# Four fused layers on one Trainium2 core: how the attention loads its images and weights, takes its first split, and places two steps of its plan

## The chip, the core and the metric

The kernel runs on one core of one Trainium2 chip. A core has a matrix engine (TensorE, PE in the profile), a vector engine (VectorE, DVE), an engine for activation functions (ScalarE, ACT), a general engine (GpSimd, POOL) and one that mostly issues transfers (SyncE, SP). SP, ACT and POOL each have a queue of DMAs, written SPq, ACTq and POOLq. Every engine works through its own instructions in order and waits on semaphores for the others. The metric is the device time of one execution in microseconds (us), lower is better: the median of three runs.

## What is computed

Four layers in a row on x of 8 images x 256 channels x 32 x 32 pixels. Layer 0 is an attention with a batch norm ahead of it and a small network behind it; layers 1 to 3 are convolutions, two of them deformable. The change touches layer 0's attention alone. Cut to that:

```python
NH, KD, D = (16, 16, 64)              # heads, width of q and k, width of v
y = _bn(xf, g1, b1)                   # mean and variance over all images and pixels
q = einsum('bcn,oc->bon', y, wq) + bq          # 256 outputs: 16 heads of 16
k = einsum('bcn,oc->bon', y, wk) + bk
v = einsum('bcn,oc->bon', y, wv) + bv          # 1024 outputs: 16 heads of 64
attn = softmax(einsum('bhnk,bhkm->bhnm', q, k) / KD ** (-0.5), axis=-1)
o = einsum('bhnm,bhmd->bhnd', attn, v)
xf = xf + einsum('bdn,od->bon', o, wp) + bp    # then batch norm, MLP, layers 1 to 3
```

Since the batch norm takes its mean and variance over all eight images, no projection can begin before the last image is there.

## The kernel before, in words

**Start.** Eight DMAs on SP's queue (L169) load one image of 1 MB each. vec, the packed small parameters, comes on ACT's queue (L176), and behind it wq and wk (L241): the host stores each head's 16 columns padded to 32, and the DMA takes only the 16, so its pieces have 64 bytes. Behind these are the biases of q and k (L253), 32 DMAs of 16 numbers each out of vec's memory. DVE forms each image's statistics (L284), 32 instructions of 512 columns, then the norm's scale and shift (L205 to L217, with a root on ACT, L213). wv follows on ACT's queue (L287), wp and bv on POOL's (L288, L289).

**First group.** From L621 on, the order of PE, ACT, DVE and POOL is written out by hand; SP's DMAs go where the program's text has them, as a rule. Four pieces project q and k of image 0 (L326), ACT adds the bias (L338) and rounds to bf16 (L340), both are written to memory, and rows are copied into the q and k tiles (L630). Then four pieces of values (L381, copied by L385). Then the split: each of q and k is cut into three bf16 levels whose sum is the number. The difference to level 0 is taken in place (L349), rounded to level 1 (L354), and the difference of that is level 2 (L356). The `split` calls stand behind all four value pieces (L631 to L635). The levels go through memory and are loaded as stacks of rows, `stack` (L364), 16 loads for each of two head pairs. The first block finds its score maxima in another way, with 32 matmuls on q and k themselves (L411) and 32 reductions (L414).

**The steady state.** A group is four heads of one image; there are 32 groups, and two blocks in each, one for each half (h) of the queries. A block takes eight steps, so a group takes 16; step t0 is a group's first. A step has, for the block in work: four score matmuls (L443) with exponentials on ACT (L444, in buffers e, six of them, which L440 takes), two pairs of value matmuls (L455), and two sums of exponentials on POOL (L463, L465). It also finds maxima for a block eleven steps ahead: eight bf16 matmuls on the stacks (L398) and four reductions on DVE (L402).

**The plan.** All other work is put by `plan(step, place, f, ...)` into a step and one of three places in it; `step` (L601) plays them out. For the next group, `project_v` makes value pieces at t0 + 0, 1, 2 and 4, `stack` loads pair 0 at t0 + 1 to 3 and pair 1 at t0 + 5 to 7, and `spread` (L370) loads q and k at t0 + 9 to 12. A pair's stack is one buffer, so its loads wait until the maxima of the pair that used it are done. In groups of even number there are also `project_qk` at t0 + 8 to 14 and `split` at t0 + 10 to 18, for the group after next (q and k of two groups are projected together). For a finished block with t1 = its end: `total` (L476) sums over keys at t1 + 3, `invert` (L486) takes the reciprocal in four parts, `lay` (L494) copies them to where they are needed with eight DMAs (r), `scale` (L499) multiplies on POOL, and `add_projected` (L529, added on DVE by L535 or L537) applies wp at t1 + 13 and 15. `enter_max` (L420 to L431) writes a block's maxima into q's spare rows. For h = 1, where t1 is the t0 of the next group, before the change:

```python
plan(t1_ + ((4, 5, 6, 8) if h == 0 and n + 2 < nblk else (4, 4, 5, 6))[i], 0, invert, m, i)
at = 8 if h == 0 and n + 2 < nblk else 6
plan(t1_ + at, 2, lay, m)
plan(t1_ + at + 2, pair, scale, m, pair)
```

## Time and profile before

| what | value |
|---|---|
| median of three runs | 4313.98 us (4313.37 to 4317.53) |
| the profiled execution's own time | 4320.31 us |
| its span | 4318.5 us |
| PE / DVE / ACT / POOL busy | 3989.3 / 3037.9 / 1859.1 / 3312.7 us |
| granted PE clock, mean | 0.971 |
| first matmul of a projection | 48.24 us after the span's start |
| first value matmul of an attention step | 108 us |
| attention's end | about 2700 us |

How to read it: the page has one row for each engine with its busy time, then the span in 40 slices (a digit is tenths of a slice), DMA queues, the chain of work that ended last, and groups of instructions by line. Other views of the same trace are a timeline (start, duration, engine, line, operation, tiles, and in brackets the idle time ahead of it with what ended it), waits in total, and stretches of time with each engine's busy time. A line such as L398 is a line of the kernel; numbers in the profile of the changed kernel stand a few lines further down.

### The profile page before, as it was taken

The page shows a single profiled execution, that of the slowest core. Times are in us where ns is not written, and L with a number is a line of the kernel's source. Part 1 is how long each engine was busy: PE and PEld are TensorE (multiplying, and loading weights), DVE is VectorE, ACT ScalarE, POOL GpSimd, SP SyncE. Part 2 cuts the span into 40 slices and gives each one's busy share as a digit, 9 for nine tenths or more (in the row PEclk, how much of TensorE's full clock was granted, in tenths as well). Part 3 has the DMA queues.
Part 4 walks back from the last instruction along what each step waited for, and adds up shares of the span by engine and source line. Part 5 has one row for each costly group of instructions (what it writes and reads, how often), then busy time and mean ns, then how long its engine had stood idle before and what let it go on. Part 6 is the DMA issues. An engine that isn't in the chain of part 4 may idle for free.

```text
span 4318.5 us, 60323 instructions
## 1 busy us (share of the span) xinstructions
PE 3989.3 (92%) x20959; PEld 1546.3 (36%) x20959; DVE 3037.9 (70%) x5148; ACT 1859.1 (43%) x3329; POOL 3312.7 (77%) x2022
## 2 busy tenths in 40 slices
PE   4999999999999999999999999999899977999976
PEld 1333333333333333333333333344334433444432
DVE  5667777767767777777677676657777764777665
ACT  1545545545545555555455454423223223444321
POOL 1888888888888988888888888447777771489767
PEclk8999999999999999999999999999999998999988
DMA  5211212222122122122122121124344442000000
GB/s 156 64 53 57 71 52 64 64 54 70 56 58 71 53 60 69 55 57 75 51 61 70 52 61 50 47 77 121 115 120 120 121 129 80 5 10 15 15 15 21
DMA packets 215834, 282.59 MB, mean 65 GB/s; under 512 B 96336, under 2 KB 126560, under 8 KB 215264
## 3 DMA queue, kind: packets, MB, share of 16 engines
q1 hardware_dynamic: 177104, 199.12, 16.1%
q0 software_dynamic: 28720, 77.90, 6.0%
q8 instruction: 168, 2.75, 0.3%
q10 hardware_dynamic: 9696, 1.62, 0.2%
q14 instruction: 146, 1.20, 0.1%
HBM read 180.55 MB, written 63.82 MB: 57 GB/s over the span
## 4 chain that ended last, share of the span: by engine, by line
PE 66%; DVE 13%; POOL 7%; issue 5%; DMA 3%; SPq 3%; ACT 2%; ACTq 0%; DVEq 0%; POOLq 0%
PE av L455 18%; PE pb L398 11%; PE sc L443 10%; POOL g L876 5%; PE pb L381 5%; PE pc L1173 5%; PE pa L1357 2%; PE pb L529 2%; PE pb L326 2%; PE po L756 2%; DMA g<-table,idx 2%; SPq L494 2%; PE pm L743 2%; DVE pm L402 2%; DVE r L486 2%
## 5 line engine op out<-in xcount | busy, mean ns | idle before, releaser
L465 POOL TENSOR_TENSOR esum<-esum,e 128x1024 f32<-128x1024 f32 x762 | 1812.6, 2413 | 57.1 <-ACT e L444 56.5
L402 DVE TENSOR_REDUCE pm<-pb 128x1 f32<-128x512 f32 x2016 | 1355.1, 684 | 662.9 <-PE pb L398 658.4
L444 ACT ACTIVATE e<-sc 128x512 f32<-128x512 f32 x2048 | 1057.2, 602 | 721.4 <-PE sc L443 713.7
L455 PE MATMUL av<-e,v 128*64 128x512 f32 x4096 | 1061.6, 597 | 0.0
L398 PE MATMUL pb<-sk,sq 128*64 128x512 bf16 x4032 | 776.0, 388 | 85.0 <-DMA sk<-lev_d 30.5
L876 POOL DMA_INDIRECT g<-table,idx x576 | 551.0, 957 | 257.0 <-issue 160.7
L398 PEld LDWEIGHTS <-sq 128*64 128x64 bf16 x4032 | 267.4, 109 | 942.9 <-issue 929.0
L443 PE MATMUL sc<-q,k 32*128 32x512 f32 x4096 | 593.5, 642 | 0.7 <-ACT e L444 0.7
L463 POOL TENSOR_TENSOR esum<-e 128x1024 f32<-128x1024 f32 x127 | 302.9, 2406 | 191.9 <-ACT e L444 191.9
L455 PEld LDWEIGHTS av<-e,v 128*64 128x64 f32 x4096 | 298.1, 138 | 211.4 <-issue 120.8
L1365 POOL TENSOR_TENSOR part<-part,pr 128x512 f32<-128x512 f32 x224 | 289.7, 1295 | 66.6 <-DVE pr L1351 55.4
L1351 DVE TENSOR_TENSOR pr<-pw,v 128x512 f32<-128x512 f32 x400 | 257.9, 682 | 106.5 <-PE pw L1346 60.3
L1173 PE MATMUL pc<-xpad,wc 128*128 128x512 f32 x576 | 277.8, 609 | 4.1 <-ACT h L1178 4.1
L499 POOL TENSOR_TENSOR o<-r,o 128x512 f32<-128x512 f32 x126 | 158.8, 1271 | 153.5 <-DMA r<-r 82.1
L529 PE MATMUL pb<-o,wp 128*64 128x512 f32 x1024 | 246.0, 599 | 3.8 <-POOL o L499 3.3
L443 PEld LDWEIGHTS sc<-q,k 32*128 32x128 f32 x4096 | 164.9, 183 | 233.1 <-issue 187.3
L743 PE MATMUL pm<-y,wide 128*128 128x512 f32 x512 | 238.9, 611 | 6.2 <-DVE y L717 5.8
L756 PE MATMUL po<-hid,w 128*128 128x512 f32 x512 | 240.3, 616 | 1.8 <-DVE x L760 1.7
L381 PE MATMUL pb<-wide,y 128*64 128x256 f32 x2048 | 241.8, 379 | 0.0
L486 DVE RECIPROCAL r<-r 128x128 f32<-128x128 f32 x252 | 233.2, 936 | 0.0
L385 ACT COPY v<-pb 128x512 f32<-128x512 f32 x128 | 75.0, 586 | 266.7 <-PE pb L381 266.7
L898 DVE TENSOR_TENSOR near_p<-g,near_p 128x320 f32<-128x320 f32 (+1 forms) x384 | 177.6, 462 | 13.2
(250 smaller groups left out, 3921.2 us busy)
## 6 DMA issues: line engine op xcount, KB each, us to landing
sq<-lev_d SPq DMA_DIRECT2D x512, 64.0 KB
r<-r SPq DMA_DIRECT2D x504, 64.0 KB
sk<-lev_d SPq DMA_DIRECT2D x496, 64.0 KB
lev_d<-lev SPq DMA_DIRECT2D x180, 128.0 KB
u_d<-u SPq DMA_DIRECT2D x60, 256.0 KB
g<-table,idx POOLq DMA_INDIRECT x576, 2.7
x<-in_x SPq DMA_DIRECT2D x8, 1024.0 KB
table<-v SPq DMA_DIRECT2D x32, 256.0 KB
```

The costliest lines, as they stand in the source:

```text
L381: nc.tensor.matmul(ps[c * 64 : (c + 1) * 64, (mt % 2) * 256 : (mt % 2 + 1) * 256], ys[b][:, t, k0 : k0 + 64], wv[:, t, g * 256 : (g + 1) * ...
L398: nc.tensor.matmul(ps[c * 64 : (c + 1) * 64, :], sq[pair][:, c, q0 : q0 + 64], sk[pair][:, c, kh * HALF : (kh + 1) * HALF], start=True, st ...
L402: nc.vector.tensor_reduce(maxima[m][:, pair, qt, kh : kh + 1], ps, AX.X, ALU.max)
L443: nc.tensor.matmul(ps, k[r, kt * P : (kt + 1) * P], q[r, h * HALF : (h + 1) * HALF], start=True, stop=True)
L444: nc.scalar.activation(es[m, kt, j // 2][:, j % 2, :], ps, AF.Exp)
L455: nc.tensor.matmul(av[i * HD : (i + 1) * HD, :], vss[b, g][:, kt, j * HD : (j + 1) * HD], e[:, i, :], start=kt == 0, stop=kt == NT - 1,)
L465: eng.tensor_add(sums[m, pair], sums[m, pair], es.pop((m, kt, pair)))
L529: nc.tensor.matmul(ps[c * 64 : (c + 1) * 64, :], wp[:, 2 * g + i, o0 : o0 + 64], outs[(b, g, h), i], start=i == 0, stop=i == 1,)
L743: nc.tensor.matmul(ps, w1[:, t, i * P : (i + 1) * P], ys[b, h][:, t, :], start=t == 0, stop=t == 1)
L756: nc.tensor.matmul(pss["o", b, h, t], w2[:, j, t * P : (t + 1) * P], hids[b, h, j], start=j == 0, stop=j == 7)
L876: nc.gpsimd.indirect_dma_start(out=g[:, k, :], out_offset=None, in_=tables[b][:TR, :], in_offset=bass.IndirectOffsetOnAxis(ap=idxs[b][:, t ...
L1173: nc.tensor.matmul(S["c", b, h], wc[:, t, k, :], tap(xpads[t], k, H // 2, h * H // 2), start=t == k == 0, stop=t == 1 and k == 8,)
```

## The change

1. Images: 16 DMAs of half an image (128 channels, 0.5 MB), those of the first half of the channels on SP's queue, those of the second half on ACT's.
2. wq and wk are loaded whole, with the padding, into two e buffers, behind the images (wq on SP, wk on ACT); ACT copies out the 16 columns of each head, two copies each.
3. Biases of q and k: in place of 32 DMAs and a multiplication on DVE, eight matmuls of one column pick the rows out of vec (with `taken`, the identity's columns without the padding, copied by POOL), and ACT writes the two tiles with the scale.
4. wv, wp and bv are issued in the hand-written part, after `normed`.
5. First split: the difference goes into the other half of its buffer (`rest`) instead of over u; its stage 0 follows each projection piece, stages 1 and 2 each value piece.
6. Odd groups make their fourth value piece at t0 + 9 instead of t0 + 4.
7. For h = 1 (all such blocks but the very last, which has a path of its own), reciprocals go to t1 + 4, 5, 6, 7 (before 4, 4, 5, 6), `lay` to t1 + 8 (before 6), `scale` to t1 + 10 (before 8).

```diff
     for b in range(B):
-        nc.sync.dma_start(x[:, :, b, :], x_in[b].rearrange("(t p) h w -> p t (h w)", p=P))
+        for t in range(2):
+            eng = nc.sync if t == 0 else nc.scalar
+            eng.dma_start(x[:, t, b, :], x_in[b, t * P : (t + 1) * P].rearrange("p h w -> p (h w)"))
...
-        for dst, name in ((wq, "wqT"), (wk, "wkT")):
-            src = d[name].rearrange("(t p) (n r) -> p t n r", p=P, r=32)
-            for t in range(2):
-                nc.scalar.dma_start(dst[:, t, :].rearrange("p (n r) -> p n r", r=KD), src[:, t, :, 0:KD])
...
-        for dst, name in ((bq4, "bq"), (bk, "bk")):
-            for c in range(4):
-                src = d["vec"][:, COL[name] + c : COL[name] + c + 1].rearrange("(n r) o -> n r o", r=32)
-                for j in range(4):
-                    r0 = (c % 2) * 64 + j * KD
-                    nc.scalar.dma_start(dst[r0 : r0 + KD, c // 2 : c // 2 + 1], src[j, 0:KD, :])
-        nc.vector.tensor_scalar_mul(bq4, bq4, 4.0)
...
+        for dst, name, eng in ((wq, "wqT", nc.sync), (wk, "wkT", nc.scalar)):
+            padded = ep.tile([P, 2, HALF], F32, name="e")
+            eng.dma_start(padded, d[name].rearrange("(t p) o -> p t o", p=P))
+            for t in range(2):
+                src = padded[:, t, :].rearrange("p (n r) -> p n r", r=32)[:, :, 0:KD]
+                nc.scalar.copy(dst[:, t, :].rearrange("p (n r) -> p n r", r=KD), src)
+        taken = w.tile([P, 4, KD], F32, name="taken")
+        nc.gpsimd.tensor_copy(taken, ident.rearrange("p (n r) -> p n r", r=32)[:, :, 0:KD])
+        for dst, name, scale in ((bq4, "bq", 4.0), (bk, "bk", 1.0)):
+            ps = ps_p.tile([P, 512], F32, name="pb")
+            for c in range(4):
+                nc.tensor.matmul(
+                    ps[c % 2 * 64 : c % 2 * 64 + 64, c // 2 : c // 2 + 1], taken.rearrange("p n r -> p (n r)"), col(name, c),
+                    start=True, stop=True,
+                )
+            nc.scalar.mul(dst, ps[:, 0:2], scale)
...
-                u = ep.tile([P, 2, HALF], F32, name="e")[:, 0, :]
+                both = ep.tile([P, 2, HALF], F32, name="e")
+                u, rest = both[:, 0, :], both[:, 1, :]
...
-                nc.vector.tensor_sub(u, u, lev[0])
+                nc.vector.tensor_sub(rest, u, lev[0])
...
-                    plan(t0 + (0, 1, 2, 4)[i], 1, project_v, *nxt, i)
+                    plan(t0 + (0, 1, 2, 9 if n % 2 else 4)[i], 1, project_v, *nxt, i)
...
+                at = 6 if n + 2 == nblk else 8
                 for i in range(4):
-                    plan(t1_ + ((4, 5, 6, 8) if h == 0 and n + 2 < nblk else (4, 4, 5, 6))[i], 0, invert, m, i)
-                at = 8 if h == 0 and n + 2 < nblk else 6
+                    plan(t1_ + ((4, 4, 5, 6) if at == 6 else (4, 5, 6, 8) if h == 0 else (4, 5, 6, 7))[i], 0, invert, m, i)
...
+            nc.scalar.dma_start(wv, d["wvT"].rearrange("(t p) o -> p t o", p=P))
+            nc.gpsimd.dma_start(wp, d["wpT"].rearrange("(t p) o -> p t o", p=P))
+            nc.gpsimd.dma_start(bv, d["bv"].rearrange("(t p) -> p t", p=P))
             for i in range(4):
                 project_qk(0, 0, i)
...
+                split(0, 0, i, 0)
             for i in range(4):
                 project_v(0, 0, i)
-            for i in range(4):
-                for k in range(3):
-                    split(0, 0, i, k)
+                split(0, 0, i, 1)
+                split(0, 0, i, 2)
```

## The prediction

> **What bounds the kernel now.** I read the 40 slices first: TensorE (PE) is at 9 tenths through the attention (the first 25 slices, to about 2700 us) except in slice one. So a gain must come from the start, where PE has nothing to do, or from PE's own waits. Next, the waits of the DMA queue of SyncE (SP) in the first 120 us: "who waits <- for what: us in total, times, longest".

> ```profile
> SPq L169 <- DMA wq<-in_wqT: 12.2, 1, 12.2
> SPq L169 <- DMA bq<-in_vec: 11.7, 2, 6.8
> SPq L169 <- DMA bk<-in_vec: 6.1, 2, 5.2
> ```

> The image loads stand still for transfers that have nothing to do with them[...]. The timeline of the same stretch (start, us, engine, line, tile; in brackets the idle time before):

> ```profile
> 14.66 12.32 ACTq L253 DMA_DIRECT2D bq<-in_vec  x16
> 27.02 11.28 ACTq L253 DMA_DIRECT2D bk<-in_vec  x16
> 43.09 2.47 DVE L284 BATCH_NORM_STATS2 stats<-x 128x6 f32<-128x512 f32 x4 [1.23 <-DMA x<-in_x]
> 48.24 3.30 PE L326 MATMUL pb<-y,wq 128*64 128x512 f32 x8 [48.24 <-DVE y L310]
> ```

> 32 bias loads of 16 numbers fill the ACT queue up to 38.3; the last image is seen at 43.09 and PE starts at 48.24. After that the first split and the first maxima:

> ```profile
> 56.65 0.69 DVE L349 TENSOR_TENSOR e<-e,esum 128x512 f32<-128x512 f32 x1 [7.09 <-DMA q<-e]
> 64.14 0.62 ACT L354 CAST esum<-e 128x512 bf16<-128x512 f32 x1
> 64.79 0.69 DVE L356 TENSOR_TENSOR esum<-e,esum 128x512 bf16<-128x512 f32 x1 [7.45 <-ACT esum L354]
> 71.33 0.68 DVE L414 TENSOR_REDUCE pm<-sc 128x1 f32<-128x512 f32 x1
> ```

> VectorE (DVE) waits 7.45 us because L354 stands behind four value copies on ACT, then alternates with ACT until 71.3; only then do the maxima begin. The table of stretches (length, busy us of PE, weight loads, DVE, ACT, POOL; granted clock, DMA share, GB/s):

> ```profile
> 71.33:93.84 22.51, 20.96 (x57) 7.21 (x58) 19.93 (x34) 0.66 (x1) 7.22 (x15) 0.50 0.66 111
> 108.20:2690.00 2581.80, 2498.65 (x15890) 916.42 (x15890) 1864.97 (x2905) 1314.73 (x2481) 2214.42 (x991) 1.00 0.21 60
> ```

> The maxima run at half clock. In the long stretch PE is 97% busy, GpSimd (POOL) 86%, DVE 72%. PE's own waits there, largest first:

> ```profile
> PE pb L398 <- DMA sk<-lev_d: 30.5, 16, 2.9
> PE pb L398 <- DVE x L537: 23.4, 44, 1.6
> PE pb L398 <- DVE pm L402: 13.2, 15, 1.8
> ```

> 16 waits for stacked keys, one for every second group. One of them, on SP's queue, PE and POOL:

> ```profile
> 395.40 0.42 SPq L364 DMA_DIRECT2D sk<-lev_d  x1
> 396.14 5.00 SPq L494 DMA_DIRECT2D r<-r  x8
> 401.18 0.58 SPq L364 DMA_DIRECT2D sq<-lev_d  x1
> ...
> 403.68 0.43 SPq L364 DMA_DIRECT2D sk<-lev_d  x1
> ```

> ```profile
> 406.39 0.41 PE L398 MATMUL pb<-sk,sq 128*64 128x512 bf16 x2 [1.36 <-DMA sk<-lev_d]
> ```

> ```profile
> 400.20 1.27 POOL L499 TENSOR_TENSOR o<-r,o 128x512 f32<-128x512 f32 x1 [2.70 <-PE pb L398]
> 402.69 1.26 POOL L499 TENSOR_TENSOR o<-r,o 128x512 f32<-128x512 f32 x1 [1.22 <-PE pb L398]
> ```

> Eight r transfers (the row sums' reciprocals) take SP 5.0 us just ahead of the last six stacking loads; PE wants them at 405.0 and gets them at 406.4. POOL idles 2.70 + 1.22 us for r as well: the releaser named, PE, is done long before, and r has just been issued.

> [...] two queues for the images give no bandwidth; the trace agrees (358 GB/s at 5 to 10 us with all queues, 401 GB/s at 40 to 45 with images alone). [...] The trace agrees with the fall (PE idle from 65.4 to 72.7, half clock from 68.1), but PE filled 93% of the maxima at half clock and did not get it back until 109.

> **The change, part by part.**

> *Images and weights.* 32 bias loads and the four element-wise weight loads go; 16 image loads of 0.5 MB, eight on each queue, come first, then vec, wk and wv behind them on ACT, wq on SP. [...] Bytes up to the last image: 8.39 MB and 1.05 MB of wp on POOL's queue; at 390 GB/s (between 358 and 401) 24.2 us. The first slice of 5 us moved 201 GB/s, so data starts at about 2.5: last byte at 26.7. An image of 1 MB took 4.80 us from the queue to the statistics at 38.26, of which 2.6 is data: I add 1.6, 28.3. But vec, before at the head of its queue, is now behind the images, and in DVE's new order bn_s (L186) stands ahead of the last six statistics: vec 28.5, table load 1.28 and L185 0.30: 30.1; then six statistics of 0.60 and eight small ones of about 0.07: 34.3; from statistics to PE as before, 48.24 - 45.56 = 2.7: PE at 37.0 instead of 48.2, **-11.2**. Bounds: -15 (vec not late) and -7 (340 GB/s). ACT's new work ahead of the batch norm's root: wq and wk land 1.05 MB later, 31.0; four copies (half the 0.62 of the 128x512 cast, an estimate) to 32.4, two small ones to 33.0; the root is wanted at 35.3. Hidden with 2.3 us to spare; weights later than that push PE by the same amount. Eight matmuls of one column run on an idle PE, the picking copy on an idle POOL: nothing. wv lands near 34, wanted at 45.

> *First split.* "rest" takes the other half of the buffer, so DVE no longer waits for the readers of e, and ACT casts after each value copy. ACT has its last projection piece at S+9.9 (S is PE's start; 58.09 before); the value copies follow PE at 1.73 us, the last ends at S+16.0, its cast at S+16.6, DVE's last difference at S+17.4. Before, 71.33 is S+23.1: **-5.7**. Next is DVE's chain of 32 maxima, 0.70 each. SP's stacking starts at about S+18 instead of S+23.6, and 32 loads took 15 us: there before S+39, when L398 needs them. PE's gap of 7.3 us shrinks to about 2; if the full clock lasts, the maxima take DVE's 0.60 instead of 0.70 (-3) and the 14.4 us after them lose up to 5. Bounds 0 and -8; I take 0, since small busy matmuls did not raise the clock before.

> *r two steps later for h = 1.* In SP's new order the six loads stand ahead of r: they go at 395.9, not 401.2, and land near 401 where PE wants them at 405.0. 5.3 us against waits of at most 2.9: all 16 go. 30.5 less what small waits take over: **-29** (bounds -10 and -31). POOL gets to its scaling two steps, four sums of 2.41 us, later: at 397.5 + 9.6 = 407. The fourth reciprocal (L486) is a step later, so r goes at about 401.5 to 406.5 and lands from 404 to 409: a wait of at most 2. Next late is L537's 0.3 us, which stays. The reciprocal moved to step 7 lies beside the output projection's matmuls (1.7 us, DVE idle 1.0 there); uncovered it would be 0.94 x 31 = 29 us. Spreads (L370) and maxima rows (L431) behind r on SP have four steps or more.

> *Fourth value piece to step 9 in odd groups.* The same 16 matmuls, 1.73 us, five steps later, still seven steps ahead of their use, and one ACT copy with them. PE doesn't wait for anything at step 4: 0. It fills the place of the stall at step 9 and so gives POOL its time back. Uncovered it costs 1.7 x 15 = 26 us.

> **Sum:** -11.2 - 5.7 - 29 = -45.9. The profiled execution took 4320.3 us (span 4318.5 and 1.8 around it): 4274. The median of the three runs is 4314.0, 6.3 below it: 4268.

> **Rivals.** *Another wait takes the stall's place* (0.13): without stalls PE asks POOL for sums faster; for it speak POOL's 86%, and 14 sums of 2.41 and two scalings of 1.27, 36.3 us, against 36.6 us of PE for the eight steps of an odd group's second half (400.1 to 436.8 on PE's rows, stall included); against it that the value piece (1.73) takes the stall's place in just that half, and 5.8 us of slack per block on average (14% of 41.5). The third part gives 12: 4285. *The clock holds through the maxima* (0.20): 8 more, 4260. *The loads don't get faster* (0.12), [...] vec is late: first part -3, 4276. *Slower* (0.05): r, behind the stacking loads and a later reciprocal, comes too late for POOL, whose sums are queued behind the scaling in order; the six e buffers fill, ACT's exponentials and PE stop. It decides where POOL waits more than its 5.8 us per block plus 45.9 / 31 = 1.5, so above 7.3 us; at 10 us it is 31 x 4.2 = 130 more: 4398. Against it: r lands at 409 at the latest by my count.

> **Numbers.** Likeliest 4268 (0.50, itself 4258 to 4278). The range takes in the clock case, the bounds of the first part and the rival with 12: 4253 to 4292. A measurement here can tell about 0.2%, 8.6 us, from no change: faster 0.92, same 0.03 (the far end of the first rival), slower 0.05.

> **What would show it.** PE's first projection matmul (L326 before) at 37 (33 to 41); the first maximum 17 to 18 us after it; no wait of PE for sk in the long stretch, L537's waits as before; POOL's idle time ahead of the scaling below 2 us; later stages unchanged in length. Wrong if PE waits for ACT's exponentials or sums instead, or if SP still issues r ahead of the stacking loads.

## The result and the profile after

The kernel after takes 4258.07 us (median of 4 runs, 4256.73 to 4258.72), the kernel before, measured beside it, 4315.75 (4 runs, 4313.37 to 4321.76): 57.7 us less, ratio 0.9864 with an interval of 0.9847 to 0.9881. The profiled execution of after took 4256.73 us, its span is 4254.9 against 4318.5 before: 63.6 us less between the two executions that can be compared line by line. The lines of the changed file stand 2 to 9 further down: L403 is L398 of before, L460 is L455, L504 is L499, L542 is L537.

**The start.** The timeline of after (start, us, engine, line, tile; in brackets the idle time before):

```profile
0.73 16.88 ACTq L171 DMA_DIRECT2D x<-in_x  x8
19.92 0.34 ACTq L178 DMA_DIRECT2D vec<-in_vec  x1
28.48 1.28 ACT L187 ACT_TABLE_LOAD   x1 [28.48 <-DMA vec<-in_vec]
30.11 0.20 DVE L188 RECIPROCAL bn_s<-bn_s 128x7 f32<-128x7 f32 x1 [4.11 <-ACT bn_s L187]
37.12 3.68 PE L330 MATMUL pb<-y,wq 128*64 128x512 f32 x8 [7.55 <-DVE y L314]
55.75 0.68 DVE L419 TENSOR_REDUCE pm<-sc 128x1 f32<-128x512 f32 x1
```

On SP's queue the images wait for no small load any more (30.0 us at L169 for wq, bq and bk in before), only for one another (L171 for x, 13.2 us, 4 times). vec is seen behind them at 28.48, DVE waits 4.11 us for the root that is made of it, PE starts at 37.12 (48.24 before), and the first maximum is at 55.75 (71.33).

**The long stretch.** Two rows of the table of stretches, from the first value matmul of an attention step to the last one (start and end, length, busy us of PE, weight loads, DVE, ACT, POOL; granted clock, DMA share, GB/s), first of before, then of after:

```profile
108.00:2744.10 2636.10, 2552.28 (x16168) 932.85 (x16166) 1904.79 (x2946) 1344.23 (x2537) 2265.08 (x1013) 1.00 0.21 60
```

```profile
92.00:2686.60 2594.60, 2540.16 (x16166) 929.68 (x16164) 1895.55 (x2946) 1342.10 (x2537) 2263.30 (x1012) 1.00 0.22 61
```

It is 41.5 us shorter. (The last value matmul of before stands at 2744, so the attention ends later than the rough 2700 given above.) Take PE's busy time off the length and 83.8 us of idle time are left before, 54.4 after: 29.4 less. But PE is also busy 12.1 us less, with the same matmuls. PE's waits in that stretch of after (in total, times, longest):

```profile
PE pb L403 <- DVE x L542: 23.5, 44, 1.6
PE pb L403 <- ACT u L343: 11.7, 14, 1.0
PE pb L403 <- DVE pm L407: 11.6, 9, 1.5
```

The row for sk (30.5 us, 16 times) is gone and no new one has come. One of the small rows took a little over: the waits for u were 7.2 us (6 times) in before, those for pm 12.8. POOL's waits ahead of the scaling in the same stretch, the two largest of before and the only one of after:

```profile
POOL o L499 <- DMA r<-r: 78.1, 30, 6.3
POOL o L499 <- PE pb L398: 58.4, 27, 4.2
```

```profile
POOL o L504 <- DMA r<-r: 3.2, 5, 1.1
```

These 137 us of waiting (150 with two smaller rows) have become 3. POOL did not gain that time: its waits for exponentials ahead of its sums grew from 248 to 354 us, so the waiting has moved to a place where PE does not wait for it. The timeline of an odd group of after shows why r is no longer late: it goes out behind the last stacking loads, and POOL, which comes to it 12 us after the first of its DMAs went out, finds it there.

```profile
380.31 5.00 SPq L499 DMA_DIRECT2D r<-r  x8
392.06 2.49 POOL L504 TENSOR_TENSOR o<-r,o 128x512 f32<-128x512 f32 x2
```

The difference between the two profiled executions, piece by piece: start to PE's first projection -11.1, from there to the first value matmul -4.9, the attention stretch -41.5, from its end to the next layer's first matmul -1.3, the rest -4.8: together -63.6.

### The profile page after: what moved, and what is told of

Read it like the earlier page. It is cut to its first block, busy times and chain, and to the rows that moved or that the text cites. A ratio compares the mean times of both kernels' runs of the same rounds, so it can differ in the third digit from the quotient of the medians.

```text
span 4254.9 us, 60310 instructions
## 1 busy us (share of the span) xinstructions
PE 3972.3 (93%) x20975; PEld 1542.8 (36%) x20975; DVE 3026.9 (71%) x5147; ACT 1858.0 (44%) x3335; POOL 3313.3 (78%) x2023
## 4 chain that ended last, share of the span: by engine, by line
PE 72%; DVE 13%; POOL 7%; issue 4%; DMA 3%; ACT 2%; SPq 0%; DVEq 0%; POOLq 0%; ACTq 0%
PE av L460 20%; PE pb L403 12%; PE sc L448 11%; PE pb L386 5%; PE pc L1182 5%; POOL g L885 5%; PE pb L534 3%; PE pa L1366 2%; PE pb L330 2%; PE pm L752 2%; PE po L765 2%; DMA g<-table,idx 2%; DVE pm L407 2%; PE pw L1355 2%; DVE r L491 1%
## 5 line engine op out<-in xcount | busy, mean ns | idle before, releaser
L460 PE MATMUL av<-e,v 128*64 128x512 f32 x4096 | 1054.2, 593 | 0.0
L403 PE MATMUL pb<-sk,sq 128*64 128x512 bf16 x4032 | 773.2, 387 | 56.3 <-DVE x L542 23.5
L403 PEld LDWEIGHTS <-sq 128*64 128x64 bf16 x4032 | 266.7, 109 | 911.5 <-issue 887.0
L460 PEld LDWEIGHTS av<-e,v 128*64 128x64 f32 x4096 | 295.0, 137 | 208.1 <-issue 117.3
L907 DVE TENSOR_TENSOR near_p<-g,near_p 128x320 f32<-128x320 f32 (+1 forms) x384 | 177.3, 462 | 13.2
L911 DVE TENSOR_TENSOR samp<-samp,near_p 128x320 f32<-128x320 f32 (+1 forms) x384 | 174.0, 453 | 13.2
```

The lines of the kernel that those rows point to most:

```text
L403: nc.tensor.matmul(ps[c * 64 : (c + 1) * 64, :], sq[pair][:, c, q0 : q0 + 64], sk[pair][:, c, kh * HALF : (kh + 1) * HALF], start=True, st ...
L460: nc.tensor.matmul(av[i * HD : (i + 1) * HD, :], vss[b, g][:, kt, j * HD : (j + 1) * HD], e[:, i, :], start=kt == 0, stop=kt == NT - 1,)
```

## The experiments

All are told in one table: first projection, first maximum and first value matmul (us), length of the attention stretch, PE's waits for sk in it (us, times), its half-clock windows, and the median less that of before on the same chip. A window is a piece of the clock's record at half speed that begins in the stretch (up to 20 us ahead of its end); one of 3.4 us at 35 to 37 us after the first value matmul, which all kernels have, is left out here (the last section comes back to it).

| kernel | projection | maximum | value | stretch | waits for sk | windows | median |
|---|---|---|---|---|---|---|---|
| before | 48.2 | 71.3 | 108.0 | 2636.1 | 30.5 (16) | 5 | |
| after | 37.1 | 55.8 | 92.0 | 2594.6 | 0 | 0 | -57.7 |
| e1_r_later | 49.4 | 72.5 | 109.1 | 2593.7 | 0 | 0 | -41.9 |
| e2_v_piece | 51.9 | 75.9 | 112.6 | 2646.4 | 31.7 (18) | 4 | +12.4 |
| e3_r_and_v | 51.6 | 75.6 | 112.2 | 2595.1 | 0 | 0 | -42.5 |
| e4_start_split | 37.5 | 54.9 | 90.7 | 2636.6 | 31.3 (17) | 3 | -17.0 |
| e5_split | 48.6 | 66.8 | 102.6 | 2635.9 | 30.8 (18) | 4 | * |
| e6_vec_first | 33.4 | 50.6 | 86.5 | 2593.2 | 0 | 0 | * |
| e7_one_queue | 35.5 | 52.7 | 88.7 | 2593.7 | 0 | 0 | * |
| e8_bias_only | 44.0 | 68.0 | 104.6 | 2630.8 | 30.4 (18) | 3 | * |
| e9_pair_recip | 37.5 | 54.8 | 90.7 | 2604.8 | 0 | 0 | -50.7 |
| e10_spare_before | 51.6 | 75.9 | 112.5 | 2800.7 | 88.5 (16) | 30 | +160.7 |
| e11_spare_after | 37.2 | 55.7 | 91.4 | 2595.0 | 0 | 0 | -60.8 |
| e12_vec_first_again | 33.4 | 50.8 | 86.6 | 2593.5 | 0 | 0 | -64.3 |

(*) These four ran on a chip on which before itself took 4652.16 us, because the layers behind the attention took longer there, by 320 to 340 us in the traces of these four; their times scatter by 17 us and more, so only their traces up to the attention's end are used. Their ratios were 0.9988 (0.9973 to 1.0003), 0.984 (0.9817 to 0.9863), 0.9856 (0.983 to 0.9882) and 0.9986 (0.997 to 1.0002).

### r two steps later, alone

```diff
+                at = 6 if n + 2 == nblk else 8
...
-                    plan(t1_ + ((4, 5, 6, 8) if h == 0 and n + 2 < nblk else (4, 4, 5, 6))[i], 0, invert, m, i)
-                at = 8 if h == 0 and n + 2 < nblk else 6
+                    plan(t1_ + ((4, 4, 5, 6) if at == 6 else (4, 5, 6, 8) if h == 0 else (4, 5, 6, 7))[i], 0, invert, m, i)
```

> The kernel before with only the reciprocals and r of h = 1 later (part 7). My theory, 'r stood ahead of the stacking loads': PE's waits for sk (30.5 us, 16 times) go, and since the half-clock windows before stand at the longest of these waits, they go too, about 8 us more: 33 to 39 us less than before. The rival 'POOL takes the stall's place' (without the value piece at step 9 POOL has no time back): 10 to 20 us less, with PE waiting for POOL or for exponentials instead. First value matmul of the attention unchanged at 108 us.

Ratio 0.9901 (0.9886 to 0.9916), 41.9 us less; the stretch is 42.4 shorter, and the waits for sk and the five windows are gone. In the stretch no wait of PE for POOL or for exponentials has taken their place: the rival falls. It is 3 us more than the most that I expected. Set step by step against before (511 steps in each trace), the 16 steps with a wait for sk are 39.3 us shorter. Of these, 30.5 are the waits themselves, and 8 are what the five steps with a half-clock window took beyond their wait. Another 2.9 stand near the attention's end, where before had one more window (17 us ahead of the end, so not counted in the table) behind a wait of 0.67 for exponentials.

### The value piece, alone and with r

```diff
-                    plan(t0 + (0, 1, 2, 4)[i], 1, project_v, *nxt, i)
+                    plan(t0 + (0, 1, 2, 9 if n % 2 else 4)[i], 1, project_v, *nxt, i)
```

> The kernel before with only the fourth value piece of odd groups at step 9 (part 6). My theory: the piece is PE work of 1.73 us whichever step it stands in, and it stands behind the maxima that wait for sk, so it cannot cover them; PE comes to these maxima 1.73 us earlier, but so do the reciprocals and with them r and the loads: within 8 us of before, the waits for sk still there 16 times. The rival 'the move of the value piece brings the 12 us that my sum lacks': 10 to 15 us less than before. A third: the loads do not come earlier, and each of the 16 waits grows by up to 1.7 us: up to 27 us more.

12.4 us slower, ratio 1.0028 (1.0021 to 1.0035), and the stretch is 10.3 longer. None of the three expectations describes it: the third allows for the number, but the waits for sk grew by 1.2 us only. The step by step comparison shows the place: step 4 of 15 odd groups is 1.73 us shorter, as it must be, step 9 longer by about the same, and step 5 is 0.70 longer in each, 10.5 in all. First e2_v_piece around such a step, then the same place in before:

```profile
389.86 1.75 DVE L486 RECIPROCAL r<-r 128x128 f32<-128x128 f32 x2
392.21 0.41 PE L398 MATMUL pb<-sk,sq 128*64 128x512 bf16 x2 [0.52 <-DVE pm L402]
```

```profile
382.82 1.89 PE L381 MATMUL pb<-wide,y 128*64 128x256 f32 x16
383.64 1.75 DVE L486 RECIPROCAL r<-r 128x128 f32<-128x128 f32 x2
```

Two reciprocals fall into step 4 and hold DVE for 1.75 us. In before PE makes the value piece just then, which wants nothing of DVE; without it PE runs on into maxima whose buffers DVE has not yet freed.

Parts 6 and 7 together, on the kernel before:

> The kernel before with parts 6 and 7, start and first split as before. My theory: the same as part 7 alone, within 4 us, so 33 to 41 us less than before. The rival 'POOL is the bound and the value piece gives its time back': 15 us or more less than part 7 alone.

Ratio 0.9895 (0.988 to 0.9911), 42.5 us less, within 1 us of r alone; the stretch is 1.4 longer. With the reciprocals spread over four steps the value piece is neither needed at step 4 nor of use at step 9. The control takes the kernel after and puts two reciprocals back into one step:

```diff
-                    plan(t1_ + ((4, 4, 5, 6) if at == 6 else (4, 5, 6, 8) if h == 0 else (4, 5, 6, 7))[i], 0, invert, m, i)
+                    plan(t1_ + ((4, 4, 5, 6) if at == 6 else (4, 5, 6, 8) if h == 0 else (4, 4, 5, 6))[i], 0, invert, m, i)
```

> The kernel after with the reciprocals of h = 1 at 4, 4, 5, 6 again (lay and scale stay two steps later, the value piece stays at step 9). My theory from the run with part 6 alone: two reciprocals of 0.94 us in one step hold up DVE's maxima, and only the fourth value piece's 1.73 us on PE covers that; without it PE waits 0.5 us and runs 0.7 us longer at step 5 of each odd group: 15 x 0.70 = 10 us more in the attention stretch, 2605 instead of 2594.6. Rival 'the 10 us of part 6 alone came from r and the stacking loads': no difference, 2594 to 2597.

2604.8 against 2594.6: 10.2 us longer, as expected; by the times of one chip 4267.85 against 4257.76 for e11_spare_after, whose stretch is that of after. The waits for sk stay gone with the reciprocals paired, so it is the later place of r that removes them, not the spreading. Part 6 costs 10 us without the spreading of part 7, and 1.4 us of the stretch at most with it.

### Only start and first split

The kernel after with parts 6 and 7 undone.

> The kernel after with parts 6 and 7 undone, so parts 1 to 5 alone (start and first split). My theory: the parts add; 16 to 18 us less than before, all of it ahead of the first value matmul of the attention (92 instead of 108 us), and waits for sk as before. The rival 'the deformable stages gain from it as well': 22 us or more less than before.

17.0 us less (ratio 0.9954, 0.9941 to 0.9968), as expected, and the stretch as in before. With the 42.5 of parts 6 and 7 that makes 59.5, against 57.7 and 60.8 in the two comparisons of the whole change: the parts add. The first split alone, on the kernel before:

```diff
+                both = ep.tile([P, 2, HALF], F32, name="e")
+                u, rest = both[:, 0, :], both[:, 1, :]
...
-                nc.vector.tensor_sub(u, u, lev[0])
+                nc.vector.tensor_sub(rest, u, lev[0])
...
+                split(0, 0, i, 0)
             for i in range(4):
                 project_v(0, 0, i)
-            for i in range(4):
-                for k in range(3):
-                    split(0, 0, i, k)
+                split(0, 0, i, 1)
+                split(0, 0, i, 2)
```

> The kernel before with only the first split changed (part 5). My theory: ACT casts right behind each value copy, so the first maximum comes 17.4 to 18.6 us after PE's first projection instead of 23.1, and all later work comes 4.5 to 5.7 us earlier; the maxima still run at half clock. Rival 'the clock holds once PE's gap of 7.3 us is gone': 8 us more, 13 us in all. Rival 'the time is lost again at the first stacked keys': no difference at the first value matmul.

From PE's start to the first maximum 18.2 us (23.1 before), to the first value matmul 54.0 (59.8): 5.8 less. PE's gap ahead of the maxima is down from 7.15 to 1.22 us. The half clock still comes, 5.6 us into the maxima, and lasts from 70.6 for 34 us, so the rival falls: with PE's gap all but closed the clock still fell.

### What the start owes to what

Before with the 32 bias loads replaced by eight matmuls, no more:

```diff
-                for j in range(4):
-                    r0 = (c % 2) * 64 + j * KD
-                    nc.scalar.dma_start(dst[r0 : r0 + KD, c // 2 : c // 2 + 1], src[j, 0:KD, :])
...
+                nc.tensor.matmul(
+                    ps[c % 2 * 64 : c % 2 * 64 + 64, c // 2 : c // 2 + 1], taken.rearrange("p n r -> p (n r)"), col(name, c),
+                    start=True, stop=True,
+                )
...
```

> The kernel before with only the 32 bias loads replaced by eight matmuls (part 3); images, weights and their queues as before (wv moves ahead, since the loads in front of it are gone). My theory [...]: the 17.8 us of waits of L169 for bq and bk go, the one for wq stays in part, and PE starts at 38 to 42 instead of 48 to 52. Rival 'the element-wise weight loads are what delays the images': PE starts at 46 or later. In both the rest is as before.

PE started at 44.0, between what my theory and the rival gave. The images' waits for bq and bk are gone, and the next late thing shows, in the waits and the timeline of this run:

```profile
SPq L169 <- DMA wq<-in_wqT: 13.0, 2, 12.6
```

```profile
1.22 13.44 ACTq L241 DMA_DIRECT2D wq<-in_wqT  x2
20.02 0.20 DVE L186 RECIPROCAL bn_s<-bn_s 128x7 f32<-128x7 f32 x1 [19.06 <-ACT bn_s L185]
26.93 13.73 DVE L289 BATCH_NORM_STATS2 stats<-x 128x6 f32<-128x512 f32 x23
```

Issuing the element-wise weights, 13.44 us for wq alone, keeps ACT from vec's root, DVE's statistics stand behind that root in order, and from 20 us on DVE works them off without a pause, up to 40.7. So the biases were worth 4 to 8 us (the kernels with the old start began at 48.2 to 51.9) and the rest of the new start the other 7. The waits above name the weight loads; how these 7 us divide among the parts of the new start was not tried.

The kernel after with all images on one queue:

```diff
-            eng = nc.sync if t == 0 else nc.scalar
+            eng = nc.sync
```

> The kernel after with all 16 image loads on SP's queue (vec, and in the built order wv too, then come first on ACT's). My theory: [...] images come no later than by wv's 1 MB, 2.7 us, and vec is early: PE starts at 35 to 38, within 2 us of the kernel after. Rival 'two queues load faster': the last image is 5 us or more later and PE starts at 41 or later.

PE started at 35.5, 1.6 earlier than in after: vec is early now, and wv's 1 MB is loaded among the images. Against e6_vec_first below, with vec early too but two queues and wv late (33.4), it is 2.1 later, less than the 2.6 that 1.05 MB take at 400 GB/s (an estimate from the rate of before at 40 to 45 us). All queues together moved 391 GB/s from 3 to 28.5 us here, with one queue for the images, and 390 in e6_vec_first, with two. The second queue is not what makes the loads faster.

The kernel after with vec ahead of the images (the two lines of vec moved up):

> The kernel after, but with vec issued ahead of the images on ACT's queue instead of behind them. My theory: vec behind the images costs the 4.11 us that DVE waited for its root in the kernel after, so PE starts at about 33 instead of 37.1, and the run is 3 to 4 us below the kernel after: 60 to 62 us below before. Rival 'the weights behind the images, or ACT's copies of them ahead of the norm's root, set the start': PE still at 35.5 to 37, 0 to 1.5 us.

PE started at 33.4: the theory's 33. The timeline of this run:

```profile
19.29 1.28 ACT L187 ACT_TABLE_LOAD   x1 [19.29 <-DMA x<-in_x]
23.96 6.61 DVE L293 BATCH_NORM_STATS2 stats<-x 128x6 f32<-128x512 f32 x11
```

ACT now starts on the root as soon as it has issued its images, and DVE's last statistics follow one another without a wait. The same kernel once more, on a chip that ran like that of after:

> The kernel after with vec ahead of the images, once more, to have its time on another chip. My theory: first projection at 33.4, and 3.5 to 5.5 us below the kernel after, 62 to 66 us below before (ratio 0.985 to 0.986). Rival 'the gain of the start is lost later': 58 to 60 us below before.

4254.22 us (4250.75 to 4257.67), 64.3 below before, ratio 0.9853 (0.9837 to 0.987), PE again at 33.4. Beside e11_spare_after, which runs like after, it is 3.5 us lower on the same chip; the single times of the two overlap, so it is the trace that shows the gain, not the times. It has the lowest time of this study.

### The price of a wait in the stretch

Eight more DMAs of the reciprocals into memory that nobody reads, for each block of h = 1, put into the kernel before and into the kernel after:

```diff
+        spare = dram.tile([P, HALF], F32, name="spare")
...
+            if m[2] == 1:
+                for j in range(8):
+                    nc.sync.dma_start(spare[16 * j : 16 * j + 16, :], rows[m][16 * j : 16 * j + 16, :])
             rows[m] = wide_rows
```

> The kernel before with eight more DMAs on SP's queue for each block of h = 1, which write the reciprocals to a spare place in memory that nobody reads, between r and the last stacking loads. About 8 x 0.40 = 3.2 us more on SP ahead of these loads. My theory: each of the 16 waits for sk grows by 3.2, from 30.5 to about 82 us in all, and each costs a half-clock window of 3.41 us or two, 1.7 us each, so PE is busy 19 us longer or more: 70 to 95 us more in the attention stretch. Rival 'only the waits count, the clock does not': 51 us more, with PE's busy time as before. Second rival 'SP had slack ahead of these loads': less than 20 us more.

160.7 us slower, ratio 1.037 (1.0353 to 1.0388), far beyond what I expected. Waits and timeline of this run:

```profile
PE pb L398 <- DMA sk<-lev_d: 88.5, 16, 6.5
PE pb L398 <- DMA u_d<-u: 50.6, 14, 4.4
```

```profile
424.87 0.64 PE L398 MATMUL pb<-sk,sq 128*64 128x512 bf16 x2 [5.05 <-DMA sk<-lev_d]
425.26 1.95 PE L455 MATMUL av<-e,v 128*64 128x512 f32 x4
```

The waits for sk grew by 58 us, 3.6 for each of the 16; eight such DMAs take 3.8 us on SP (my 3.2 was too low). A wait that I had not thought of came with them: in 14 even groups PE waits for the writes of u, 50.6 us, which the spare DMAs seem to hold up on SP. And each of the 30 waits is followed by half clock: four value matmuls take 1.95 us in place of 1.02. PE was busy 2610.0 us in the stretch, 57.7 more than in before. These three terms come to 166, about the 165 us by which the stretch grew. So the clock is paid, as the theory says; the part of u was missing in both.

> The kernel after with the same eight spare DMAs behind r. My theory: what counted was that r stood ahead of the stacking loads, not how much SP has to do: the attention stretch stays at 2594.6 within 4 us. Rival 'SP's queue is full and the spreads and maxima rows behind r come late': 20 us or more.

2595.0 us, and no new wait: 60.8 below before (ratio 0.986, 0.9844 to 0.9877), like after. The same eight DMAs that cost 165 us of the stretch ahead of the stacking loads cost nothing behind them.

## Why the prediction was right, and where it was not

*Images and weights* (predicted -11.2): -11.1. The inner steps hold too: the last image bytes on SP's queue at 26.6 (26.7 predicted), vec's root done at 30.1, the last statistics at 34.3, PE at 37.1. That vec, issued behind the images on ACT's queue, would land behind them was my assumption, shown by no row of before; here it came out so: the last image packet on that queue was done at 26.9, vec's packets ran from 26.5 to 27.8. That two queues for the images give no bandwidth is borne out by e7_one_queue (391 GB/s with one, 390 in e6_vec_first with two).

*First split* (-5.7): -4.9 in the two profiles, -5.8 alone in e5_split. The clock's record shows full speed from 5.8 us after PE's start on, in before from 2.8; so the projections took 9.8 us up to the first value piece, in place of 8.3, and the first maximum came 18.6 us after PE's start, not 17.4. The clock did not hold through the maxima, as the likeliest case had it: half speed from 56.6 for 37.5 us.

*r two steps later* (-29, bounds -10 and -31): the mechanism is the one given. PE's idle time is 29.4 less, the place of r in SP's order is the cause (e1, e9, e10 and e11), L537's waits stay at 23.5, POOL's waits for r fell from 78.1 to 3.2. But the stretch became 41.5 shorter, outside my bounds. The term that was sized wrong is the price of a wait: I took it for its length, but PE was also busy 12.1 us less. Five of the sixteen waits had cost the clock too, about 8 us, and a sixth window, near the end and not behind a wait for sk, about 2 more; the last 2 are spread thin.

*Fourth value piece* (0): 0, but the reason was incomplete. "PE doesn't wait for anything at step 4" is true because the piece stands there; it covered the two reciprocals, and gone alone it costs 10 us (e2, e9). That it "gives POOL its time back" isn't seen: with r alone POOL waits 1.2 us ahead of the scaling, and the stretch is as short (e1 against e3).

*The rest.* I took 6.3 us off since the profiled execution of before lay that far above the median of three. Later medians of before were 4315.75 (the same three and one more), 4318.53 and 4319.61: the profiled one lies 1 to 5 us above them, so most of the 6.3 was a low draw of three, and the correction had little ground. The last 4.8 us between the profiles, mostly in layers whose code is the same, are left to such scatter: the stretch from the next layer's first matmul to the convolutions took 864.7 us in the profile of before, 860.3 in after, and 860.3 to 863.8 in the eight other kernels that ran on chips like it, with and without r moved.

So 4268 was 10 us too high, and 4258 lies at the very edge of the likeliest band. That it lies there at all is in part luck: the correction of 6.3 hid part of the miss. From the profiled execution the sum would be 4274.4, and after's is 4256.7, 17.7 less: 12.5 of it in the stretch, 1.3 at its end, 4.8 in the rest, less 0.9 in start and split. The rivals: no other wait took the stall's place, the clock did not hold, the loads did get faster, and r did not come too late for POOL.

## What to carry to other kernels

Read the order of a DMA queue like that of an engine: a transfer that nobody wanted yet cost nothing here at the end of the queue (e11), and 165 us ahead of one that was awaited (e10). Price a wait of the busiest engine with what follows it, here the clock (with it, PE was busy 57.7 us longer in e10), and not with its length alone. Before moving work away, ask what else runs during it: a piece that waits for nothing may be the cover of another engine's work.

## What the runs showed of the hardware

```profile
238.88 0.64 PE L398 MATMUL pb<-sk,sq 128*64 128x512 bf16 x2 [2.19 <-DMA sk<-lev_d]
239.27 1.95 PE L455 MATMUL av<-e,v 128*64 128x512 f32 x4
```

```profile
1223.21 0.41 PE L403 MATMUL pb<-sk,sq 128*64 128x512 bf16 x2 [2.54 <-DMA sk<-lev_d]
1223.42 1.05 PE L460 MATMUL av<-e,v 128*64 128x512 f32 x4
```

The wait of 2.19 us lies almost whole in one cell (2.08), and the matmuls after it are slow; the longer one, of 2.54, is cut into 1.11 and 1.44 by a cell's border and cost nothing more. In before the five waits with 2.08 to 2.51 us in one cell were each followed by half clock, one with 2.01 was not.

Waits are not the whole of it. The window that all kernels have at 35 to 37 us into the stretch follows a cell in which PE was never idle, but spent 1.95 us on 16 matmuls of one column (here in e5_split, where L456 is L455 of before):

```profile
135.64 1.95 PE L301 MATMUL pb<-bv,wp 128*128 128x1 f32 x16
139.37 1.91 PE L456 MATMUL av<-e,v 128*64 128x512 f32 x4
```

The same 16 matmuls come once more, 43 us later. In all 14 traces the first set lay whole in one cell and was followed by half clock, and the second was cut by a border, with at most 1.55 us in one cell, and was not. So these matmuls went with the clock's fall as a wait of their length did, though the profile counts them as busy. The first maxima, matmuls on 16 rows, fit this: in e5_split PE was idle only 1.1 us in the cell ahead of the fall at 70.6, and in the cells after it PE was busy without a break and stayed at half clock. These are readings of the traces; how the hardware counts was not tried by itself.
